# Loading and normalising the first token block tile by tile, with identity products ahead of it and another order of the first projections

## Chip, cores and metric

The kernel runs on one core of one Trainium2 chip. The metric is the device time of one execution in microseconds (us). The time of the kernel before is the median of three runs.

## What is computed

A sandwich of a differential-attention layer and a feed-forward layer over 2048 tokens of width 256, all in float32. Cut to what matters here:

```python
x = x + layernorm(attention(layernorm(x)))
x = x + layernorm(ffn(layernorm(x)))

# attention, 16 query heads and 8 key heads of width 128, in pairs
q, k, v = split(h @ Wqkv.T + b)
p = softmax(causal(q1 @ k1.T)) - lam * softmax(causal(q2 @ k2.T))
lam = exp(sum(lq1 * lk1)) - exp(sum(lq2 * lk2)) + LAMBDA_INIT
o = rmsnorm(p @ v) * subln_w * (1 - LAMBDA_INIT)
return concat(o) @ out_w.T + out_b
```

The change is in the first tenth of the kernel: the first layer norm, and the projections to q, k and v of the first tokens.

## The kernel before

The 16 query heads are worked in four groups g of four, each with two key heads and one value head of width 256. Tokens come in four blocks b (or nb) of 512, each of four tiles t of 128. For each block the kernel loads `xt` (128 partitions, 4 tiles, 256 columns), normalises it in place (`norm_in`, L462), turns it with eight TensorE transposes into `xnT` (`turn_in`, L468), and projects it: `project_heads` (L166) makes two heads of 512 tokens, `project_values` (L196) the values. In `project_heads` part 0 and part 1 are the query heads, part 2 the two key heads; `put_block` (L725) calls the values part 3.

A layer norm is `rstd_of` (L84): `bn_stats` and `bn_aggr` on VectorE for each tile (L89, L90), one addition of eps for all (L92), one power of -1/2 on GpSimd for all (L94). Then `normalise` (L97, L98) subtracts and scales tile by tile on VectorE.

In `turn_in` the eight transposes (L475) write one PSUM tile `pst`; ScalarE copies its first half (L476), then VectorE its second (L477).

**PSUM buffers.** Projections, turned tokens and scores share one pool `ps_s` of three buffers (tag "sc"), taken in turn: whatever is made first in the code gets the next buffer, and waits until the tile made three places earlier has been read. Projections of q and k are read by ScalarE (L192, with `both=False` both halves), those of v by VectorE (L209), scores by VectorE (L270, L281).

**Attention.** A `Unit` is one pair of heads for one tile of 128 queries. Short units (i under 8) hold two half tiles of queries (`subs` 0 and 1), and `scores(u, half)` works them in two halves; unit 0 has scores of 64 keys in its first half and of 128 in its second, unit 1 of 192 and 256. After the scores come exponentials on ScalarE (L298), the combination of the two maps (L325), which needs the scalar `nlam`, a transpose through DRAM (L347, L349, L359), and products with v three steps later (L371).

**What sets the order.** `manual_schedule` is on: each engine executes its instructions in the order in which the Python code issues them, and waits at each for its inputs. The main loop takes one unit a step. Projections and norms are hung into it by `put` into four dictionaries: `before` (ahead of the step's scores), `mid` and `between` (in this order, after the first half of the scores and its exponentials, ahead of the second half) and `after`. Step 0 reads in the kernel before:

```python
put(before, 0, norm_in, 0)
put(before, 0, load_lambdas)
put(before, 0, turn_in, 0)
put_block(before, [0] * 2, 0, 0, [2, 0], both=False)
put(before, 0, norm_in, 1)
put(before, 0, turn_in, 1)
put_block(before, [0] * 2, 0, 0, [1, 3], both=False)
put(before, 0, norm_in, 2)
```

**Loads.** SyncE's queue issues the four `xt` loads of 512 KB (L457); the fourth has to wait until the first buffer is free. ScalarE's queue issues the weights of group 0 (`load_qkv`, L131): two pieces of q, then k, then v, of 256 KB each (L137, L141). GpSimd's queue issues the columns of constants (L459), the bias of v (L142), and, in `load_lambdas` (L481 to L487), the lambda vectors `lt`, the output weights `wo` and two constants. `lambdas` (L489) works out `nlam`: VectorE multiplies and sums, ScalarE takes two exponentials (L498), VectorE subtracts (L499) and scales `wo` (L157). In the kernel before it stands after the values of block 1.

A matmul of the program in float32 stands in the profile as two TensorE instructions, a transpose as one: four matmuls of `project_heads` are eight records of L174, eight transposes of `turn_in` eight records of L475.

Of the kernel before, what the change touches and what calls it, by code (L numbers as in the profile page):

```python
# [10 lines left out]
F32 = mybir.dt.float32  # L11
# [5 lines left out]
P = 128  # L17
# [13 lines left out]
LAMBDA_INIT = 0.8 - 0.6 * math.exp(-0.3 * 1)  # L31
SCALE = D ** (-0.5)
LAG = 3
MASKED = -1e30
LOWEST = -3e38

# [10 lines left out]
def kernel(  # L47
# [16 lines left out]
    nc = tc.nc  # L64

    const = ctx.enter_context(tc.tile_pool(name="const", bufs=1))
    ident = const.tile([P, P], F32, name="ident")
    make_identity(nc, ident)
    hadm = const.tile([P, P], F32, name="hadm")

    make_causal_mask(nc, hadm, MASKED)
    mask = const.tile([P, 64], F32, name="mask")
# [11 lines left out]
    def rstd_of(pool, src, n, tag):  # L84

        st = pool.tile([P, 4, 6], F32, tag="st" + tag, name="st" + tag)
        mv = pool.tile([P, 4, 2], F32, tag="mv" + tag, name="mv" + tag)
        for t in range(n):
            nc.vector.bn_stats(st[:, t, :], src[t] if isinstance(src, list) else src[:, t, :])  # L89
            nc.vector.bn_aggr(mv[:, t, :], st[:, t, :])  # L90
        ve = pool.tile([P, 4], F32, tag="ve" + tag, name="ve" + tag)
        nc.vector.tensor_scalar(ve[:, :n], mv[:, :n, 1], EPS, None, ALU.add)  # L92
        rstd = pool.tile([P, 4], F32, tag="rs" + tag, name="rs" + tag)
        nc.gpsimd.tensor_tensor(rstd[:, :n], ve[:, :n], mhalf[:, :n], ALU.pow)  # L94
        return mv, rstd

    def normalise(dst, src, mv, rstd, t):  # L97
        nc.vector.tensor_scalar(  # L98
            dst, src, mv[:, t, 0:1], rstd[:, t : t + 1], ALU.subtract, ALU.mult
        )  # L100

    x4 = x.rearrange("(b t p) d -> b p t d", p=P, t=4)
# [5 lines left out]
    with ExitStack() as actx:  # L108
# [6 lines left out]
        ps_s = actx.enter_context(tc.tile_pool(name="ps_s", bufs=3, space=PSUM))  # L115
# [12 lines left out]
        wsrc = wqkvT.rearrange("(c p) o -> p c o", p=P)  # L128
        loaded = {}

        def load_qkv(g, engine, pieces=1):  # L131

            wq = xtp.tile([P, 2, 1024], F32, tag="wq", name=f"wq_{g}")
            vb = xtp.tile([P, 256], F32, tag="vb", name=f"vb_{g}")
            step = 512 // pieces
            for lo in range(0, 512, step):
                engine.dma_start(  # L137
                    wq[:, :, lo : lo + step], wsrc[:, :, g * 512 + lo : g * 512 + lo + step]
                )
            for lo, at in ((512, 2048 + g * 256), (768, 3072 + g * 256)):  # L140
                engine.dma_start(wq[:, :, lo : lo + 256], wsrc[:, :, at : at + 256])  # L141
            nc.gpsimd.dma_start(vb, vbias[:, ts(g, 256)].to_broadcast([P, 256]))  # L142
            loaded[g] = wq, vb

# [308 lines left out]
        xsm = pstack.enter_context(tc.tile_pool(name="xsm", bufs=2, side="right"))  # L453
        xts = []
        for b in range(NB):
            xt = xin.tile([P, 4, HID], F32, tag="xt", name=f"xt_{b}")
            nc.sync.dma_start(xt, x4[b])  # L457
            xts.append(xt)
        nc.gpsimd.dma_start(colv, cols)  # L459
        load_qkv(0, nc.scalar, pieces=2)  # L460

        def norm_in(b):  # L462
            xt = xts[b]
# [215 lines left out]
        def ffn_pieces():  # L679
            for b in range(NS - 1, -1, -1):  # L680
                prev, nxt = b + 1 < NS, b > 0
                if nxt:
                    load_x(b - 1)
                yield hidden(b, 0)
                if nxt:
                    front2(b - 1)
                if prev:
                    yield back(b + 1)
                    finish1(b + 1)
                    finish2(b + 1)  # L690
                yield hidden(b, 1)
                if nxt:
                    front3(b - 1)
                yield hidden(b, 2)
                if nxt:
                    turn_ffn(b - 1)
                    if b > 1:
                        front1(b - 2)
                yield hidden(b, 3)
            back(0)  # L700
            for lo in range(2):
                finish1(0, lo, 1)
                finish2(0, lo, 1)

        pieces = ffn_pieces()
# [14 lines left out]
        before, mid, between, after = {}, {}, {}, {}  # L720

        def put(where, step, f, *args, **kw):
            where.setdefault(step, []).append(lambda: f(*args, **kw))

        def put_block(where, steps, g, nb, parts, both=True):  # L725
            for step, part in zip(steps, parts):
                if part == 3:
                    put(where, step, project_values, g, nb)
                else:
                    put(where, step, project_heads, g, nb, part, both=both)  # L730


        put(before, 0, norm_in, 0)
        put(before, 0, load_lambdas)
        put(before, 0, turn_in, 0)
        put_block(before, [0] * 2, 0, 0, [2, 0], both=False)
        put(before, 0, norm_in, 1)
        put(before, 0, turn_in, 1)
        put_block(before, [0] * 2, 0, 0, [1, 3], both=False)
        put(before, 0, norm_in, 2)  # L740
        put_block(mid, [0] * 2, 0, 1, [0, 1], both=False)
        put(between, 0, turn_in, 2)
        put_block(between, [0] * 2, 0, 1, [2, 3], both=False)
        put(between, 0, lambdas)
        put(mid, 1, norm_in, 3)
        put_block(mid, [1] * 2, 0, 2, [0, 1], both=False)
        put_block(between, [1, 1], 0, 2, [2, 3], both=False)
# [3 lines left out]
        for g in range(1, NG):  # L751
            end = place[g, NT - 1, 0]
            put(after, end - 12, load_qkv, g, nc.sync)
            put(after, end + LAG + 2, load_wo, g)
            put(mid, end + LAG + 3, scale_wo, g)
            if g == 1:

                for nb in range(3):
                    put_block(between, [end + 5 - 2 * nb, end + 6 - 2 * nb], g, nb, [0, 1])
                put_block(before, [end] * 2, g, 3, [0, 1])  # L760
                for nb in range(4):
                    put_block(before, [end], g, nb, [2])
                    put_block(after, [end + 2], g, nb, [3])
            else:
                put_block(between, [end - 5, end - 4, end - 4, end - 3], g, 3, range(4))
                put_block(between, [end - 3, end - 3, end - 2, end - 2], g, 2, range(4))
                put_block(between, [end - 2, end - 1, end - 1], g, 1, range(3))
                put_block(after, [end - 1, end], g, 1, [3])
                put_block(before, [end], g, 0, [2])
                put_block(between, [end, end + 1], g, 0, [0, 1])  # L770
                put_block(after, [end + 2], g, 0, [3])
# [17 lines left out]
        for where, step, count in (  # L789
            *((between, last - 4 + j, 1) for j in range(4)),  # L790
            *((w, last + j, 1) for j in range(LAG + 3) for w in (before, between)),
            (after, last + LAG + 3, 6 * NS),
        ):
# [3 lines left out]
        at = lambda k: units[k] if 0 <= k < len(units) else None  # L797
        for step in range(len(units) + LAG + 4):
            for f in before.get(step, ()):
                f()  # L800
            new, mixed = at(step), at(step - 1)
            ripe, out1, out2, out3, out4 = (at(step - LAG - k) for k in range(5))
            if new:
# [96 lines left out]
```

## Time and profile before

| | us |
|---|---|
| median of three runs | 1495.02 |
| lowest and highest | 1494.45, 1495.09 |
| the profiled execution's own time | 1495.16 |
| its span, first to last instruction | 1493.4 |
| TensorE busy | 1454.7 (97%) |
| VectorE busy | 1080.2 (72%) |
| ScalarE busy | 498.3 (33%) |
| GpSimd busy | 285.4 (19%) |
| 16 DMA engines, queue of SyncE | 58.8% of the span |

A profile line of the timeline has: start in us from the span's start, length, engine and line, operation, output and inputs, how many instructions were merged, and in brackets the idle time of that engine before it and what ended it. PE is TensorE's matmuls, PEld its weight loads, DVE VectorE, ACT ScalarE, POOL GpSimd, SP SyncE; a q after the name is the engine's queue. The line of a table by stretches has: the stretch, its length, each engine's busy time with its number of instructions, the granted share of TensorE's clock, the DMA engines' share and GB/s. Ends of matmuls are modelled, so starts are the safer reading. The records of the granted clock begin in this trace at 17.13 us; earlier stretches are given as 1.00 for lack of a record.

### The profile page before, as it was taken

To read this page: it belongs to the slowest core of one execution; us is meant where nothing else is said; L and a number is where in the kernel's file an instruction comes from. 1 tells how busy PE (TensorE), PEld (TensorE's weight loads), DVE (VectorE), ACT (ScalarE), POOL (GpSimd) and SP (SyncE) were. 2 spreads that over 40 slices of the span, in tenths; PEclk is the share of its full clock that TensorE was granted. 3 is DMA by queue.
4 is the path that set the end of the run, shared out by engine and by line. 5 is a ranking of instruction groups with operands and counts; after the bars stand their busy time and mean duration, and the time that the engine had idled before them with its cause. 6 is when DMAs were issued, how large, how long until landed. Compare 5 with 4: busy or idle time off the path is not lost.

```text
span 1493.4 us, 17588 instructions
## 1 busy us (share of the span) xinstructions
PE 1454.7 (97%) x5464; PEld 1038.3 (70%) x5464; DVE 1080.2 (72%) x2825; ACT 498.3 (33%) x1011; POOL 285.4 (19%) x376
## 2 busy tenths in 40 slices
PE   6899999999999999999999999999999999999998
PEld 3457767666767777675677776665776666888887
DVE  3479788756666888654978788547898888866674
ACT  1354333323223334332333333324323233541211
POOL 2013222101111122111311121112221221222110
PEclk9999999999999999999999999999999999999999
DMA  3038998865366897831798888523997768622000
GB/s 115 8 93 185 186 207 171 170 127 121 77 136 151 168 201 158 164 78 50 167 180 175 172 193 178 110 64 84 245 189 159 157 160 164 144 79 64 24 26 15
DMA packets 463789, 198.41 MB, mean 133 GB/s; under 512 B 366128, under 2 KB 460864, under 8 KB 463696
## 3 DMA queue, kind: packets, MB, share of 16 engines
q1 hardware_dynamic: 459856, 187.62, 58.8%
q0 software_dynamic: 2592, 8.48, 2.1%
q10 hardware_dynamic: 1248, 1.18, 0.2%
q8 instruction: 45, 0.74, 0.2%
q14 instruction: 48, 0.39, 0.1%
HBM read 104.95 MB, written 92.27 MB: 132 GB/s over the span
## 4 chain that ended last, share of the span: by engine, by line
PE 87%; DVE 11%; issue 1%; ACT 1%; DMA 0%; POOL 0%; POOLq 0%; DVEq 0%; ACTq 0%
PE po L371 28%; PE sc L260 26%; PE pp L174 11%; PE pout L438 7%; PE gu L628 7%; PE pv L202 4%; PE pd L658 4%; DVE e L270 3%; DVE e L325 2%; DVE e L347 1%; DVE e L281 1%; DVE xo L417 0%; DMA xt<-in_x 0%; PE tx L615 0%; DVE nb L293 0%
## 5 line engine op out<-in xcount | busy, mean ns | idle before, releaser
L260 PE MATMUL sc<-k,q 128*128 128x512 f32 (+7 forms) x1280 | 481.6, 522 | 16.3 <-DVE last L281 8.9
L371 PE MATMUL po<-v,pt 128*128 128x256 f32 x2176 | 485.5, 379 | 0.0
L371 PEld LDWEIGHTS po<-v,pt 128*128 128x128 f32 x2176 | 425.7, 196 | 57.2 <-issue 10.0
L260 PEld LDWEIGHTS sc<-k,q 128*128 128x128 f32 x1280 | 237.2, 191 | 239.7 <-issue 191.7
L298 ACT ACTIVATE e<-e,nb 128x192 f32<-128x192 f32 (+28 forms) x256 | 299.5, 1170 | 302.2 <-DVE u L395 172.6
L270 DVE TENSOR_SCALAR_CACHE_REDUCE e<-sc 128x1024 f32<-128x1024 f32 (+14 forms) x248 | 231.5, 934 | 157.1 <-PE sc L260 156.4
L399 POOL TENSOR_TENSOR f<-u,mhalf 128x1 f32<-128x1 f32 (+1 forms) x96 | 59.3, 618 | 946.8 <-DVE u L395 644.7
L382 ACT COPY osb<-po 128x256 f32<-128x256 f32 (+1 forms) x96 | 42.6, 444 | 427.3 <-PE po L371 427.3
L174 PE MATMUL pp<-xnT,wq 128*128 128x512 f32 x384 | 174.5, 604 | 5.9 <-ACT xnT L476 3.0
L347 DVE STREAM_TRANSPOSE e<-e 128x768 f32<-128x768 f32 (+7 forms) x192 | 172.4, 937 | 7.1 <-DVE e L325 0.5
L401 POOL TENSOR_SCALAR osb<-osb,f 128x256 f32<-128x256 f32 x128 | 172.1, 1350 | 9.5
L325 DVE SCALAR_TENSOR_TENSOR e<-e,cf,e 128x64 f32<-128x64 f32 (+31 forms) x128 | 170.6, 1353 | 3.4
L174 PEld LDWEIGHTS pp<-xnT,wq 128*128 128x128 f32 x384 | 73.6, 194 | 90.9 <-issue 79.4
L438 PE MATMUL pout<-wo,oT 128*128 128x256 f32 x512 | 121.0, 379 | 0.0
L270 DVE TENSOR_SCALAR_CACHE_REDUCE e<-sc,mx 128x192 f32<-128x192 f32 (+13 forms) x136 | 100.5, 739 | 22.9 <-PE sc L260 9.1
L438 PEld LDWEIGHTS pout<-wo,oT 128*128 128x128 f32 x512 | 97.4, 190 | 12.8
L281 DVE CUSTOM_DVE_ANT_0 e<-sc,mask,mx 128x64 f32<-128x64 f32 x248 | 70.5, 284 | 8.9
L641 ACT ACTIVATE hT<-gu,colv 128x256 f32<-128x256 f32 x64 | 30.3, 474 | 133.7 <-PE gu L628 89.6
L628 PE MATMUL gu<-fxnT,wgate 128*128 128x256 f32 x256 | 65.8, 380 | 0.2 <-DVE last L281 0.2
L628 PE MATMUL gu<-fxnT,wup 128*128 128x256 f32 x256 | 65.7, 379 | 0.0
L642 DVE SCALAR_TENSOR_TENSOR hT<-gu,colv,hT 128x256 f32<-128x256 f32 x64 | 30.9, 482 | 40.0 <-ACT hT L641 39.9
L202 PE MATMUL pv<-wq,xnT 128*128 128x256 f32 x256 | 57.5, 380 | 0.2 <-DVE last L281 0.2
(103 smaller groups left out, 933.3 us busy)
## 6 DMA issues: line engine op xcount, KB each, us to landing
dr<-e SPq DMA_DIRECT2D x20, 1024.0 KB, 4.7
pt<-dr SPq DMA_DIRECT2D x80, 256.0 KB, 5.6
dr<-e SPq DMA_DIRECT2D x20, 896.0 KB, 4.3
pt<-dr SPq DMA_DIRECT2D x80, 224.0 KB, 5.1
do<-xo SPq DMA_DIRECT2D x64, 256.0 KB, 2.4
oT<-do SPq DMA_DIRECT2D x256, 64.0 KB, 2.7
dr<-e SPq DMA_DIRECT2D x20, 768.0 KB, 4.0
pt<-dr SPq DMA_DIRECT2D x80, 192.0 KB, 4.6
```

Source lines behind the costliest of these rows:

```text
L174: nc.tensor.matmul(pp[:, ts(h, 512)], lhsT=wq[:, c, ts(j, P)], rhs=xnT[:, c, cols4], start=(c == 0), stop=(c == 1),)
L202: nc.tensor.matmul(pp[:, ts(t, 256)], lhsT=xnT[:, c, ts(nb * 4 + t, P)], rhs=wq[:, c, 768:1024], start=(c == 0), stop=(c == 1),)
L260: nc.tensor.matmul(sc[:, lo : lo + ww], lhsT=qT[m][:, u.i, u.subs[a]].rearrange("d p q -> d (p q)"), rhs=kT[m][:, at + lo : at + lo + ww], ...
L270: nc.vector.tensor_scalar(e[:, at : at + full], sc[:, :full], 1.0, best, ALU.mult, ALU.max, accum_out=u.mx[:, k0, c : c + 1],)
L281: nc.vector.tensor_tensor_reduce(e[:, L - 64 : L], sc[:, full : full + 64], mask, 1.0, best, ALU.add, ALU.max, accum_out=u.last[:, k0 : k0 ...
L298: nc.scalar.activation(e, e, AF.Exp, bias=u.nb[:, 2 * a + m : 2 * a + m + 1], scale=SCALE, accum_out=u.d[:, a, m : m + 1],)
L325: nc.vector.scalar_tensor_tensor(e0, e1, cf[:, a : a + 1], e0, ALU.mult, ALU.add)
L347: nc.vector.transpose(xv[:, r], ev[:, r])
L371: nc.tensor.matmul(u.po[:, ts(a, HID)], lhsT=ptv[:, g, r, :], rhs=vt[:, kc, :], start=(kc == 0), stop=(kc == u.i),)
L401: nc.gpsimd.tensor_scalar(u.osb[:, a, :], u.osb[:, a, :], f[:, a : a + 1], None, ALU.mult)
L438: nc.tensor.matmul(u.pout[:, :HID], lhsT=u.oT[:, c, p, :], rhs=wos[u.g][:, p, c, :], start=(p == 0 and c == 0), stop=(p == 1 and c == 1),)
L628: nc.tensor.matmul(ps[:, ts(2 * j + n, 256)], lhsT=ffn[which][:, c, ts(fc, P)], rhs=xnT[:, c, :], start=(c == 0), stop=(c == 1),)
```

## The change

The first block comes in four transfers of 128 KB (one tile each), two from SyncE's and two from ScalarE's queue, and the weights of group 0 are issued behind them on ScalarE's queue. `load_qkv` issues k first, then q, then v, in all groups. The first block is normalised by `norm_first`: statistics, addition and power for each tile alone, with the normalisation of a tile issued after the statistics of the next. `warm_up` multiplies the identity with itself twelve times into a buffer of `ps_s` that nothing reads. In step 0, `lambdas` comes after the norm of block 1 and ahead of part 1 of q; `turn_in` of block 1 comes after part 1 instead of ahead of it; the values of block 0 and the norm of block 2 come after the first scores.

```diff
+WARM = 12
...
-            for lo in range(0, 512, step):
-                engine.dma_start(
-                    wq[:, :, lo : lo + step], wsrc[:, :, g * 512 + lo : g * 512 + lo + step]
-                )
-            for lo, at in ((512, 2048 + g * 256), (768, 3072 + g * 256)):
-                engine.dma_start(wq[:, :, lo : lo + 256], wsrc[:, :, at : at + 256])
+            parts = [(512, 2048 + g * 256, 256)]
+            parts += [(lo, g * 512 + lo, step) for lo in range(0, 512, step)]
+            parts += [(768, 3072 + g * 256, 256)]
+            for lo, at, n in parts:
+                engine.dma_start(wq[:, :, lo : lo + n], wsrc[:, :, at : at + n])
...
-            nc.sync.dma_start(xt, x4[b])
+            if b:
+                nc.sync.dma_start(xt, x4[b])
+            else:
+
+                for t in range(4):
+                    (nc.sync, nc.scalar)[t % 2].dma_start(xt[:, t, :], x4[0][:, t, :])
+                load_qkv(0, nc.scalar, pieces=2)
             xts.append(xt)
         nc.gpsimd.dma_start(colv, cols)
-        load_qkv(0, nc.scalar, pieces=2)
+
+        def warm_up():
+
+            warm = ps_s.tile([P, 1024], F32, tag="sc", name="warm")
+            for k in range(WARM):
+                nc.tensor.matmul(warm[:, :P], lhsT=ident, rhs=ident, start=True, stop=True)
+
+        def norm_first():
+
+            xt = xts[0]
+            done = None
+            for t in range(4):
+                ln = rstd_of(xsm, xt[:, t : t + 1, :], 1, f"x{t}")
+                if done:
+                    normalise(xt[:, t - 1, :], xt[:, t - 1, :], *done, 0)
+                done = ln
+            normalise(xt[:, 3, :], xt[:, 3, :], *done, 0)
...
-        put(before, 0, norm_in, 0)
+        put(before, 0, warm_up)
+        put(before, 0, norm_first)
         put(before, 0, load_lambdas)
         put(before, 0, turn_in, 0)
         put_block(before, [0] * 2, 0, 0, [2, 0], both=False)
         put(before, 0, norm_in, 1)
+        put(before, 0, lambdas)
+        put_block(before, [0], 0, 0, [1], both=False)
         put(before, 0, turn_in, 1)
-        put_block(before, [0] * 2, 0, 0, [1, 3], both=False)
-        put(before, 0, norm_in, 2)
+        put_block(mid, [0], 0, 0, [3], both=False)
+        put(mid, 0, norm_in, 2)
         put_block(mid, [0] * 2, 0, 1, [0, 1], both=False)
         put(between, 0, turn_in, 2)
         put_block(between, [0] * 2, 0, 1, [2, 3], both=False)
-        put(between, 0, lambdas)
```

## The prediction

> **What bounds the kernel now.** I read the table of stretches first: from 100 us on TensorE is busy 99 us in 100, so what the first 55 us lose is lost for good, and what they win shifts the rest. There I read the timeline, by engine. First the start:
>
> ```profile
> 0.73 11.41 SPq L457 DMA_DIRECT2D xt<-in_x  x4
> 5.64 0.43 DVE L89 BATCH_NORM_STATS2 stx<-xt 128x6 f32<-128x256 f32 x1 [5.64 <-DMA xt<-in_x]
> 7.90 0.17 DVE L92 TENSOR_SCALAR vex<-mvx 128x4 f32<-128x4 f32 x1
> 8.23 1.05 POOL L94 TENSOR_TENSOR rsx<-vex,mhalf 128x4 f32<-128x4 f32 x1 [4.82 <-DVE vex L92]
> 9.31 1.45 DVE L98 TENSOR_SCALAR xt<-xt,mvx,rsx 128x256 f32<-128x256 f32 x4 [1.24 <-POOL rsx L94]
> 9.78 1.97 PE L475 MATMUL pst<-ident,xt 128*128 128x128 f32 x8 [9.78 <-DVE xt L98]
> 11.78 0.58 ACT L476 COPY xnT<-pst 128x512 f32<-128x512 f32 x1 [6.92 <-PE pst L475]
> 12.42 9.45 PE L174 MATMUL pp<-xnT,wq 128*128 128x512 f32 x16 [0.68 <-ACT xnT L476]
> ```
>
> A strict chain: the block lands at 5.62, norm, transposes, copy, and the first projection starts at 12.42. Next, TensorE's clock, from the weight loads:
>
> ```profile
> 16.00 0.33 PEld L174 LDWEIGHTS pp<-xnT,wq 128*128 128x128 f32 x1 [0.52 <-issue]
> 16.85 0.33 PEld L174 LDWEIGHTS pp<-xnT,wq 128*128 128x128 f32 x1 [0.52 <-issue]
> 17.42 0.19 PEld L174 LDWEIGHTS pp<-xnT,wq 128*128 128x128 f32 x1 [0.24 <-issue]
> 17.85 0.19 PEld L174 LDWEIGHTS pp<-xnT,wq 128*128 128x128 f32 x1 [0.24 <-issue]
> ```
>
> Starts lie 0.85 us apart until 17.13 (the first clock record) and 0.43 after it: half a clock for 4.7 us of projections, a loss of 2.35. Then TensorE's own order, with the waits in brackets:
>
> ```profile
> 21.71 1.04 PE L475 MATMUL pst<-ident,xt 128*128 128x128 f32 x8
> 30.95 3.70 PE L174 MATMUL pp<-xnT,wq 128*128 128x512 f32 x8 [0.93 <-DVE v L209]
> 36.00 3.70 PE L174 MATMUL pp<-xnT,wq 128*128 128x512 f32 x8 [1.35 <-DVE last L281]
> 48.78 0.59 PE L260 MATMUL sc<-k,q 128*128 128x192 f32 x2 [0.87 <-DVE v L209]
> 51.43 0.98 PE L260 MATMUL sc<-k,q 128*128 128x192 f32 x2 [2.06 <-DVE e L270]
> ```
>
> Each is a wait for a PSUM buffer that VectorE has still to read: 5.21 us. At 36.00 VectorE reads the first scores late, since the norm of block 2 is queued ahead of them; at 51.43 `lambdas` is. The last wait also costs clock (0.59 us busy in 3.35, then 0.50 granted):
>
> ```profile
> 47.91:51.26 3.35, 0.59 (x2) 0.30 (x2) 3.01 (x12) 0.20 (x1) 0.00 (x0) 1.00 0.00 0
> 51.26:54.67 3.41, 3.24 (x5) 1.82 (x6) 3.06 (x22) 1.86 (x8) 0.00 (x0) 0.50 0.01 2
> ```
>
> That is 3.24/2 = 1.62 more.
>
> **What the Trainium skill says.** "TensorE: Matmul & The Clock Gate", Part 1, section "What's actually happening": the array runs at half rate until a free-running window of about 3.4 us was busy, and falls back after an idle one. The trace agrees: the slow stretch is 3.41 long, 17.13 and 51.26 are ten such stretches apart. How busy a window must be isn't said; here 17% lost the clock. The same page, Part 4, says that transposes don't count as busy in the same way; no run so far tests that. "DMA: Bandwidth & Descriptors", section "Issuing engines are not separate DMA queues": transfers of all queues share the same 16 engines, so two queues save issue time only. The trace agrees: one issue takes about 0.5 us, and block and weights land together (5.62, and 5.3 for the first weights).
>
> **The change, part by part.**
>
> *Four transfers.* The DMA view gives 83, 60 and then about 350 GB/s in slices of 0.75 us from 1.5 us on, so 107 KB by 3.0 us; 131 KB, one tile, is there at 3.1. The whole block lands 0.5 to 0.8 us after its bytes can have moved (block plus first weights, 786 KB, are there at 4.9). I take 3.9 for the landing of tile 0, range 3.6 (alone) to 4.3 (tile 1 shares the engines). Tiles 1 to 3 follow within 1.2 us at that rate and are needed 0.8, 2.0 and 3.1 later: covered. k's 256 KB are behind 512 KB on the two queues, some 8 us, and needed at 10.4: 2.4 us of cover.
>
> *Norm by tile.* From the block's rows statistics to aggregate takes 0.46, aggregate to addition 0.22, addition to the next statistics 0.12. The power of one column stands at the kernel's end:
>
> ```profile
> 1484.65 0.15 DVE L92 TENSOR_SCALAR vec<-mvc 128x1 f32<-128x1 f32 x1
> 1484.95 0.55 POOL L94 TENSOR_TENSOR rsc<-vec,mhalf 128x1 f32<-128x1 f32 x1 [12.97 <-DVE vec L92]
> 1485.53 0.54 DVE L98 TENSOR_SCALAR y<-pd,mvc,rsc 128x256 f32<-128x256 f32 x1 [0.73 <-POOL rsc L94]
> ```
>
> so addition to normalisation takes 0.88. After tile 0 lands, its normalisation starts at 1.60 (behind tile 1's statistics), each next at 1.16 more (0.36 + 0.46 + 0.22 + 0.12): 2.76, 3.92; the last waits for its own power, 3.12 + 0.68 + 0.88 = 4.68. In the block it was 9.31 + 3×0.36 − 5.62 = 4.77: four powers instead of one eat the overlap. What is won is that only two transposes are left: 0.47 to the first (as 9.31 to 9.78), 0.21 + 0.42 at half clock, 0.67 for the copy. The first projection starts at 3.9 + 4.68 + 0.47 + 0.63 + 0.67 = 10.35, against 12.42: **2.07**.
>
> *Identities.* 12 products are 24 records. At half clock transposes of this size come 0.21 apart (8 in 1.97, the last 0.42 long), so 5.1 us, from 1.45 (identity ready, after POOL's masks) to 6.6; the first transposes are due at 5.97 and the last pair at 9.05, so this is hidden. Upper bound: 0.33 each, the weight load's length at half clock: 7.9, to 9.4. What they buy is open: between 7.5 and 10.35 only four transposes run, so a clock won at 7 can be lost again. I value the identities at nothing, with one slow stretch of 3.4 us from the first projection, 1.7; bounds 0 (clock held) and 2.6. Sixteen records at full clock took 21.71 − 12.42 − 2.35 = 6.94; turn of block 1 or part 1 can follow at 10.35 + 6.94 + 1.7 = 18.99 instead of 21.71. With the landing: **2.7**, of which 0.65 is clock.
>
> *New order.* Let E be the end of part 1 (18.99 + 3.43 = 22.4).
> - Transposes of block 1 run from E to E+0.87. ScalarE copies q's halves at E+0.2 to 1.46 (1.26 for two), then `pst` to 2.05; VectorE's half ends at 2.75. First scores: the second needs q's other half, 0.2 us idle. Values need the buffer of `pst` (three places back): 2.85 instead of 1.88, 0.97 idle. This is new; part 1 covered it before.
> - VectorE reads the first scores right behind that copy (E+3.1), so both waits in front of block 1's queries (0.93, 1.35) go. The norm of block 2 runs on VectorE from E+7.7 to 12.6; its transposes are due at 13.2: covered by 0.6.
> - `lambdas` (2.1 us of VectorE) moves behind the norm of block 1, near 16. It waits for ScalarE's exponential, which is behind the copies of part 0, E−2.0; done at E−0.8, and VectorE owes nothing until E+2.05: 2.8 us of cover. Its loads stay behind the powers on POOL: the fourth starts at 8.5, as the one did at 8.23, so they land as before (lt 4.5 after issue, wo 5.3: by 15). `lambdas`' going leaves the wait at 48.78 (0.87) and nearly removes the next: 0.1. With 2.06 less idle, TensorE keeps its clock.
>
> Before 5.21 + 1.62 = 6.83; after 0.2 + 0.97 + 0.87 + 0.1 = 2.14: **4.7**. The part loaded first in later groups comes 12 steps ahead: nothing.
>
> Sum 2.7 + 4.7 = 7.4. The profiled execution took 1495.16 (1493.4 span, 1.76 around it): 1487.8. It stands 0.14 above the median of 1495.02: **1487.6**.
>
> **Rivals.**
> 1. The clock holds from the identities to the projections: 1.7 more, 1485.9. For: 5 us of products fill a window. Against: little runs between 7.5 and 10.35.
> 2. The first block gains little: identities at 0.33 end at 9.4, eight transposes follow at 0.21, the first projection starts near 12.0; or tile 0 lands with the old block, 5.62, and it starts at 12.07. 7.4 − 1.7 = 5.7: 1489.3. Against: SyncE's first bytes move by 2 us.
> 3. The clock drop moves instead of going: another wait (71.01 to 73.39 is 2.4 us idle) falls into a window whole. 7.4 − 1.6 = 5.8: 1489.2. The windows are free-running, so this is chance; the drop at 1252.75 may as well vanish.
> 4. Slower: `lambdas` now stands on VectorE ahead of block 1's copy and all scores. If lt or wo landed late, everything would queue behind. Its cover ends if wo lands after about 23.5; to eat 7.4 it must land after 31, against 15 before. That decides from 16 us of delay.
>
> **Numbers.** Forecast 0.50 (own range 1486.3 to 1488.8), rival 1 0.20, rivals 2 and 3 together 0.24, change without effect 0.04, rival 4 0.02. The range runs from clock held and tile 0 at 3.6 with a little spared later (1485.1) to rivals 2 or 3 with a late landing (1490.2). A measurement tells 0.2%, 3.0 us, from no change; all but the last two cases lie beyond: faster 0.94, same 0.04, slower 0.02.
>
> **What would show it.** First statistics near 3.9 and first projection near 10.35; weight loads 0.85 apart for four records there, then 0.43; a wait of about 1 us ahead of the values of block 0, none ahead of block 1's queries, unit 1's second scores close behind its first and no clock drop there. A first projection at 12, or a drop that stands elsewhere, would make me wrong by 1.7; a wait on VectorE's `lambdas` for a DMA would by more.

## The result, and the profile after

| | before | changed |
|---|---|---|
| median of six runs each, us | 1495.16 | 1488.29 |
| lowest to highest | 1494.45 to 1496.82 | 1485.62 to 1489.19 |
| the profiled execution's own time | 1495.16 | 1489.19 |
| its span | 1493.4 | 1487.4 |

The ratio is 0.9948 with a 95% interval of 0.9935 to 0.9961: 6.9 us less. The forecast was 1487.6. The two profiled executions differ by 6.0 (the changed one is the slowest of its six), and these 6.0 can be followed from start to end. First the timeline of the changed kernel at its start, in the order of the data:

```profile
1.46 4.28 PE L471 MATMUL warm<-ident 128*128 128x128 f32 x24 [1.46 <-POOL ident masks.py:199]
3.95 0.43 DVE L90 BATCH_NORM_STATS2 stx<-xt 128x6 f32<-128x256 f32 x1 [3.95 <-DMA xt<-in_x]
8.53 0.41 DVE L99 TENSOR_SCALAR xt<-xt,mvx,rsx 128x256 f32<-128x256 f32 x1 [0.44 <-POOL rsx L95]
9.48 0.59 ACT L498 COPY xnT<-pst 128x512 f32<-128x512 f32 x1 [2.05 <-PE pst L497]
10.36 2.15 PE L174 MATMUL pp<-xnT,wq 128*128 128x512 f32 x3 [0.92 <-DMA wq<-in_wqkvT]
```

The first statistics start at 3.95 instead of 5.64, the last normalisation 4.58 later, the first projection at 10.36 instead of 12.42. Its bracket names what came last: a DMA, k's weights, not ScalarE's copy. The copy of `xnT` started 0.64 ahead of the first projection in the kernel before (11.78 to 12.42); by that measure the projection could have started at 10.12, and the weights cost 0.24 here.

Next the table of stretches of the changed kernel; the share of the clock is the column after the five engines:

```profile
7.71:11.13 3.42, 1.65 (x6) 0.89 (x7) 1.48 (x4) 0.59 (x1) 3.05 (x5) 1.00 1.07 346
11.13:14.54 3.41, 3.41 (x5) 1.33 (x4) 2.26 (x9) 0.00 (x0) 0.55 (x1) 0.50 1.03 343
65.74:69.15 3.41, 3.28 (x4) 1.50 (x5) 1.01 (x4) 0.08 (x1) 0.15 (x1) 0.50 0.23 77
```

The records of the granted clock in this trace begin at 4.30, while the identities ran: full clock from there. It was lost again at 11.13, after a window in which TensorE ran the last transposes and 0.77 us of projections, and came back 3.41 later. It was lost once more at 65.74, after a wait that the change does not touch. TensorE's timeline shows where that is:

```profile
25.15 3.72 PE L202 MATMUL pv<-wq,xnT 128*128 128x256 f32 x16 [0.77 <-DVE xnT L499]
28.71 7.03 PE L174 MATMUL pp<-xnT,wq 128*128 128x512 f32 x16
...
44.82 1.12 PE L260 MATMUL sc<-k,q 128*128 128x192 f32 x4 [0.87 <-DVE v L209]
45.85 10.54 PE L174 MATMUL pp<-xnT,wq 128*128 128x512 f32 x24
...
62.46 1.04 PE L497 MATMUL pst<-ident,xt 128*128 128x128 f32 x8
65.87 2.07 PE L174 MATMUL pp<-xnT,wq 128*128 128x512 f32 x2 [2.37 <-ACT xnT L498]
```

One wait is new (0.77 ahead of block 0's values). The queries of block 1 (28.71) follow without a wait, and so do the second scores of unit 1 (44.82, four records in one group). Blocks 2 and 3 start at 45.85 and 65.87 instead of 52.20 and 73.39. The same two starts, in TensorE's timeline of the kernel before:

```profile
52.20 8.26 PE L174 MATMUL pp<-xnT,wq 128*128 128x512 f32 x16
...
73.39 3.78 PE L174 MATMUL pp<-xnT,wq 128*128 128x512 f32 x8 [2.37 <-ACT xnT L476]
```

So the account of the two traces is: 2.71 less at the end of the first sixteen projection records (19.00 for 21.71; the end is taken as the start of the record behind them), 7.52 less at block 3 (the kernel before had paid its clock drop at 51.26 by then), and 6.0 less at the end. The difference of 1.5 is the drop at 65.74, which the trace before does not have.

### The profile page after: what moved, and what is told of

Read it like the earlier page. It is cut to its first block, busy times and chain, and to the rows that moved or that the text cites. A ratio compares the mean times of both kernels' runs of the same rounds, so it can differ in the third digit from the quotient of the medians.

```text
span 1487.4 us, 17643 instructions
## 1 busy us (share of the span) xinstructions
PE 1458.2 (98%) x5488; PEld 1040.3 (70%) x5488; DVE 1080.8 (73%) x2828; ACT 498.6 (34%) x1011; POOL 287.1 (19%) x379
## 4 chain that ended last, share of the span: by engine, by line
PE 86%; DVE 11%; DMA 1%; issue 1%; ACT 1%; ACTq 0%; SPq 0%; POOL 0%; POOLq 0%; DVEq 0%
PE po L371 28%; PE sc L260 25%; PE pp L174 11%; PE gu L650 7%; PE pout L438 7%; PE pd L680 4%; PE pv L202 4%; DVE e L270 3%; DVE e L325 2%; DVE e L347 2%; DVE e L281 1%; DMA wq<-in_wqkvT 1%; DVE xo L417 0%; PE tx L637 0%; DVE nb L293 0%
## 5 line engine op out<-in xcount | busy, mean ns | idle before, releaser
L371 PEld LDWEIGHTS po<-v,pt 128*128 128x128 f32 x2176 | 425.3, 196 | 57.6 <-issue 10.2
```

The costliest lines, as they stand in the source:

```text
L371: nc.tensor.matmul(u.po[:, ts(a, HID)], lhsT=ptv[:, g, r, :], rhs=vt[:, kc, :], start=(kc == 0), stop=(kc == u.i),)
```

## The experiments

Unless a table says otherwise, the edit is made to the changed kernel, and everything is still computed. "Block 2" and "block 3" are the starts of their first projections, as above. The medians with an interval were taken against the kernel before on the same chip.

**The head alone, the order alone.** `e1_head` keeps loads, norm and identities of the change, and takes step 0 of the kernel before:

```diff
-put(before, 0, norm_in, 0)
+put(before, 0, warm_up)
+put(before, 0, norm_first)
```

> The changed head (four transfers, norm by tile, identities, k's weights first) with the old order of step 0. If head and order add up, the first projection starts at 10.4 us and the turn of block 1 at 19.0 instead of 21.7, the four waits for PSUM buffers (5.2 us together) and a clock drop behind the last of them come back, and the time is about 2.7 us under the kernel before: near 1492.4. Rival: the earlier start is given back at the old waits (VectorE's norm of block 2 and lambdas are late anyway); then the first projection is early but the projections of block 2 start within 0.5 us of the 52.2 of before, and the time is that of before.

`e2_order` is the kernel before with the other half:

```diff
 put(before, 0, norm_in, 1)
+put(before, 0, lambdas)
+put_block(before, [0], 0, 0, [1], both=False)
 put(before, 0, turn_in, 1)
-put_block(before, [0] * 2, 0, 0, [1, 3], both=False)
-put(before, 0, norm_in, 2)
+put_block(mid, [0], 0, 0, [3], both=False)
+put(mid, 0, norm_in, 2)
...
-put(between, 0, lambdas)
```

> The old head with the new order of step 0. If they add up: first projection at 12.4, part 1 starting at 21.7, a wait of about 0.8 ahead of the values of block 0, none at block 1's queries, projections of block 2 starting near 48.6 instead of 52.2 and at full clock, so 4.7 to 4.9 us under before, near 1490.3; 1.6 more where a clock drop falls into another wait. Rival: the order pays only with the early head, because lambdas then waits for its loads or the norm of block 2 is late; then a new wait on VectorE of over 1 us stands in the first 50 us and the gain is under 3.

| | first projection | 16 records done | block 2 | block 3 | median us | ratio to before, interval |
|---|---|---|---|---|---|---|
| before | 12.42 | 21.71 | 52.20 | 73.39 | 1495.16 | |
| changed | 10.36 | 19.00 | 45.85 | 65.87 | 1488.29 | 0.9948, 0.9935 to 0.9961 |
| e1_head | 10.29 | 18.72 | 49.15 | 71.63 | 1493.09 | 0.9975, 0.9967 to 0.9983 |
| e2_order | 12.35 | 21.08 | 47.93 | 67.95 | 1490.78 | 0.9966, 0.9953 to 0.9978 |

By the medians the two halves add up within their intervals: 0.25% and 0.34%, against 0.52% together. At block 2 they seem to give too much, 3.05 from the head and 4.27 from the order, where the change has 6.35. The surplus of 0.97 lies at the start, where the first stretch of half clock fell otherwise: e1 has its sixteen records done 0.28 ahead of the changed kernel, e2 0.63 ahead of the kernel before. Behind the sixteen records the parts separate cleanly. In e1 the stretch from there to block 2 is 30.43 long, as before (30.49), with nearly the same waits in it (0.93, 1.28, 0.87, 2.06): a head gained 3 us early is not eaten at the next wait. In e2 it is 26.85, exactly that of the changed kernel. To block 3 it is 51.68 in the kernel before, and 46.87 in both the changed kernel and e2. So the order brings 4.81, and the remaining 2.71 of the 7.52 stand at the end of the sixteen records.

**What in the order counts.** `e4_lambdas_back` puts `lambdas` back to where the kernel before had it:

```diff
-put(before, 0, lambdas)
...
 put_block(between, [0] * 2, 0, 1, [2, 3], both=False)
+put(between, 0, lambdas)
```

> The changed kernel with lambdas back at its old place, behind the values of block 1. Theory: VectorE does its 2.1 us of lambdas between the values of block 1 and unit 1's scores again, so the wait in front of unit 1's second scores comes back at about 2.0 us, and the projections of block 2 start at 47.9 instead of 45.85; where a clock window holds that wait whole, the clock drops behind it (1.6 more). Rival: the norm of block 2, not lambdas, makes that wait; then it stays under 0.3 and the start is 45.9.

TensorE's timeline of e4:

```profile
45.31 0.98 PE L260 MATMUL sc<-k,q 128*128 128x192 f32 x2 [2.06 <-DVE e L270]
46.08 11.63 PE L174 MATMUL pp<-xnT,wq 128*128 128x512 f32 x24
```

The wait of 2.06 is back, to the hundredth, and the stretch from the sixteen records to block 2 is 29.25 instead of 26.85: 2.4 more. Near the end of the wait the clock fell, at 45.0, as it had at 51.26 in the kernel before; that is why the 24 records from 46.08 take 11.63 instead of 10.54. A single run took 1488.99 us beside 1494.73 of the kernel before. That is no worse than the changed kernel although a wait of 2 us is back, because in this run the clock held from 7.45 to 45.0, the sixteen records were done at 16.83, and no drop fell at block 3.

`e8_values_ahead` puts the values of block 0 ahead of the first scores again:

```diff
-put_block(mid, [0], 0, 0, [3], both=False)
+put_block(before, [0], 0, 0, [3], both=False)
```

> The changed kernel with the values of block 0 ahead of the first scores again, but behind the turn of block 1, and the norm of block 2 still behind the scores. Theory: the values behind the scores bring nothing themselves: ahead, their own wait (0.77) goes, and a wait of 0.9 for VectorE's reading of them stands before block 1's queries; the 1.3 us wait for the scores stays away, since that was the norm of block 2. Projections of block 2 start at 45.7 to 46.0, less what the clock does at the start. Rival: the values' place is what pays, both old waits (0.9 and 1.3) come back and block 2 starts at 47 or later.

```profile
29.05 7.13 PE L174 MATMUL pp<-xnT,wq 128*128 128x512 f32 x16 [0.93 <-DVE v L209]
```

This is TensorE's timeline of e8 at block 1's queries: the wait of 0.93 that the change had removed is back, and the one of 0.77 that it had brought is gone. From the sixteen records to block 2 it takes 26.49, against 26.85. Behind or ahead of the scores, the values cost one wait of this size. The 1.28 to 1.35 of the kernel before are gone in e8 too: that is the work of the norm of block 2 alone, which stands behind the first scores in both.

**The loads and the norm.** `e6_one_transfer` and `e7_block_norm` undo one each:

```diff
 # e6
-for t in range(4):
-    (nc.sync, nc.scalar)[t % 2].dma_start(xt[:, t, :], x4[0][:, t, :])
+nc.sync.dma_start(xt, x4[0])
```

```diff
 # e7
-put(before, 0, norm_first)
+put(before, 0, norm_in, 0)
```

> The changed kernel, but the first block comes in one transfer of 512 KB on SyncE's queue, with the weights beside it from the start; norm by tile and all else as changed. Theory: splitting the transfer is what makes the head earlier: the first statistics start at 5.6 instead of 3.95, the first projection at about 12.0 instead of 10.36, and part 1 ends 1.0 to 2.4 later (the clock moves with it). Rival: norm by tile makes the head earlier; then the first projection stays within 0.6 us of 10.4.

> The changed kernel with the block norm (one addition and one power for all four tiles) on the four transfers. Theory: the tiles land within 0.8 us, and the block norm takes as long from the first tile as the norm by tile (4.7 against 4.6 us), so the last normalisation ends at about 9.0 and the first projection still starts where k's weights land, 10.2 to 10.4. Rival: norm by tile is worth about 1 us; then the first projection starts at 11.2 or later.

With one transfer the first statistics start at 5.55 and the first projection at 11.71; a single run took 1493.17 us. That time does not price the transfers alone: the clock was lost at 11.0 for two stretches, the sixteen records were done at 21.70, and drops followed at 69.0 and 598. With four transfers and the norm of the whole block, the start of e7 is, in the timeline of TensorE:

```profile
7.55 1.48 PE L497 MATMUL pst<-ident,xt 128*128 128x128 f32 x8 [1.47 <-DVE xt L99]
9.71 10.57 PE L174 MATMUL pp<-xnT,wq 128*128 128x512 f32 x24 [0.68 <-ACT xnT L498]
```

The first statistics of e7 started at 3.42, and the copy of `xnT` 5.65 later; in the changed kernel the copy starts 5.53 behind the statistics. Beside the identities, the norm tile by tile is worth 0.1 us. Without them it is worth 0.37 (5.77 in e3 below, 6.14 in the kernel before), since the slow transposes then no longer stand in a row; both together bring 0.6. The small transfers bring the larger part (first statistics at 5.55 in e6, at 3.95 in the changed kernel). In e7 the eight transposes stood together, the clock was full from 5.02 past the first projections, and a single run took 1486.45 us.

**The identities and the clock.** `e3_no_identities` leaves them out; `e5_fill` puts 11 more products of the identity behind the transposes of the four tiles, into the same buffer that nothing reads:

```diff
 # e3
-put(before, 0, warm_up)
```

```diff
 # e5, in turn_in, behind the two transposes of tile t
+if b == 0:
+    fill((3, 3, 2, 3)[t])
```

> The changed kernel without the twelve identity products; all else the same. Theory: they buy little, since the clock they win at 4.3 us is lost at 11.1, 0.8 us into the projections: without them the last transposes take 0.25 longer, the first projection starts at 10.3 to 10.6 (it waits for k's weights anyway), all of it at half clock until a busy window ends: 0.4 to 1.3 us slower than the changed kernel, near 1489. Rival 1: they carry the head's gain, 2 us or more lost. Rival 2: nothing at all, within 0.3 us at the start of part 1.

> The changed kernel with eleven more identity products, put behind the transposes of each tile of block 0 (3, 3, 2, 3), so that TensorE is busy for most of the time up to the first projection. Theory: the clock drop at 11.1 comes from the nearly idle stretch before it, so it goes: the projections run at 0.43 us from the first on, part 1 starts at 17.3 instead of 19.0, time 1.7 us under the changed kernel, near 1486.6. Rival: products of the identity don't keep the clock, or the products delay the transposes: part 1 still starts at 19 or later.

Without identities the sixteen records were done at 19.18 (changed: 19.00), and the median is 1489.09, ratio 0.9950 (0.9936 to 0.9963). In this pair of traces the twelve products bring 0.2 us, less than the first statistics differ from one execution to the next (3.95 and 3.47), and the medians show no difference. That is no fixed price: in the changed kernel their clock is lost before the projections profit, but of the eight traces with these twelve products and four transfers it held through the sixteen records in three (e4, e7, e12), which had them done at 16.66 to 16.83, and was lost in five, at 18.72 to 20.77. With 23, TensorE's timeline reads

```profile
10.19 10.57 PE L174 MATMUL pp<-xnT,wq 128*128 128x512 f32 x24
20.59 1.04 PE L502 MATMUL pst<-ident,xt 128*128 128x128 f32 x8
```

24 records in 10.57 instead of 12.23: no drop at the start, sixteen records done at 17.16, block 2 at 44.01, both 1.84 earlier. The median, 1488.40 with ratio 0.9944 (0.9931 to 0.9956), does not show it. In its trace two drops stand later, at 64.64 and at 593.70, where the changed kernel's trace had one, at 65.74 (each has a further one near 1245). In this one trace, what the start gains and the later windows cost are of the same size.

**Other waits, and the weights.** `e10_turn_early` moves the turn of block 3 from step 2 into step 1, behind block 2's values and ahead of the scores, so that its copy is done when the projections of block 3 are due:

```diff
-put(mid, 2, turn_in, 3)
...
 put_block(between, [1, 1], 0, 2, [2, 3], both=False)
+put(between, 1, turn_in, 3)
```

> The changed kernel with the turn of block 3 moved from step 2 to step 1, behind the values of block 2. Theory: the 2.37 us wait at 63.5 us, and the clock drop that starts in it, come from ScalarE's copy of that block being queued behind unit 2's exponentials; placed earlier the copy is done in time, block 3's first projection starts near 62.7 instead of 65.9, no drop at 65.7: 2.5 to 3.2 us, and 1.6 more in executions that had the drop there. Rival: unit 2's first scores or the projection then wait for VectorE's copy instead, and under 1.5 us is won.

```profile
63.89 1.47 PE L260 MATMUL sc<-k,q 128*128 128x320 f32 x4 [0.26 <-DVE xnT L499]
65.20 3.24 PE L174 MATMUL pp<-xnT,wq 128*128 128x512 f32 x7
```

In TensorE's timeline of e10 the wait of 2.37 is gone (0.26 is left ahead of the scores), block 3 starts 17.58 behind block 2 instead of 20.02, and no drop stands near it. The median is 1484.12 (1483.71 to 1487.88), ratio 0.9928 (0.9915 to 0.9940). It is the fastest version with more than one run. The changed kernel on the same chip (e13 below) took 1488.94, so this is 4.8 less, of which the 2.44 between the two blocks are seen in the trace; the profiled execution is the slowest of the five, and what the others saved beyond that was not traced.

`e11_all` joins e5 and e10, and puts eight products of the identity behind the transposes of the feed-forward layer of the last group of blocks (`whole` is the PSUM tile that `tx` is half of), where all traces have a wait of 2.4 and a clock drop near 1245:

```diff
+for k in range(8 if b == NS - 1 else 0):
+    nc.tensor.matmul(whole[:, 512:640], lhsT=ident, rhs=ident, start=True, stop=True)
```

> The changed kernel with the eleven identity products between the first tiles, the early turn of block 3, and eight identity products behind the first transposes of the feed-forward, where TensorE waits 2.36 us at 1243.5. Theory: three clock drops go (11.1, 65.7 and 1246.8), together with most of the wait at 63.5: 1.7 + 2.5 to 3.2 + about 1.5 us under the changed kernel in the trace, near 1482.5. Rival: products that nobody reads don't hold the clock at 1243, or delay the scores behind them: no gain beyond the sum of the first two, near 1484.

```profile
1240.81 0.78 PE L260 MATMUL sc<-k,q 128*128 128x320 f32 x2 [0.57 <-DVE last L281]
...
1244.51 4.97 PE L260 MATMUL sc<-k,q 128*128 128x320 f32 x12 [1.89 <-ACT fxnT L649]
```

It missed: 1486.18 (1484.99 to 1487.17), ratio 0.9937 (0.9923 to 0.9950), not better than e10. The timeline of TensorE shows two losses. The wait ahead of 1240.81 is short now, but a new one of 1.89 stands three scores on, and the clock fell at 1244.3 all the same; from block 3 to the end it takes 1421.9, against 1420.0 in traces whose only drop is the one near 1245. And k's weights made the first projection late by 1.4 (11.13). Why the scores at 1244.51 wait for the copy of `fxnT`, which the changed kernel does not show, stays open.

`e12_bias_late` issues the bias of v of group 0 with the loads of the lambdas, behind the powers on GpSimd's queue (8.02 instead of 1.66); `e13_changed_again` is the changed kernel once more.

```diff
 def load_qkv(g, engine, pieces=1):
...
-    nc.gpsimd.dma_start(vb, vbias[:, ts(g, 256)].to_broadcast([P, 256]))
+    if g:
+        load_vb(g, vb)
...
 def load_lambdas():
+    load_vb(0, loaded[0][1])
```

> The changed kernel with the load of v's bias on GpSimd's queue moved from 1.7 us to behind the powers of the first norm. Theory: its 128 KB in 4 KB packets, moved beside the tokens and weights from 3.75 to 7.5 us, hold DMA engines and are why these stretches run at 230 GB/s instead of 361; then k's weights land by about 8.5 instead of 10.2 and the first projection waits only for the copy. Rival: the small transfers themselves are slower to feed; the rate stays under 280 and k's weights land at 10 or later.

> The changed kernel once more, as it is, to stand beside the two others on one chip. Expected 1486 to 1489 with the number of clock drops behind the start (none to three) setting which; if the drops are set by where the waits fall in free-running windows, this trace's drops lie elsewhere than at 11.1, 65.7 and 1246.8 while the starts up to the first drop agree within 0.5 us. Rival: the drops belong to the program and stand at the same places.

The first projection in TensorE's timeline, of e13 and then of e12:

```profile
11.01 13.31 PE L174 MATMUL pp<-xnT,wq 128*128 128x512 f32 x24 [2.05 <-DMA wq<-in_wqkvT]
```

```profile
9.69 10.57 PE L178 MATMUL pp<-xnT,wq 128*128 128x512 f32 x24 [0.68 <-ACT xnT L502]
```

The copy of `xnT` started at the same time in both (8.99 and 9.05), so that both first projections could start near 9.7. In e13 k's weights held it back by 1.4 us; in e12 nothing did, the clock held, and block 3 started at 63.53. In e12 the weights landed at 8.9, later than the 8.5 expected and well ahead of the rival's 10; the rate, 281 as shown below, lies just above the 280 that the rival named. A single run of e12 took 1485.36 us. The same program as the changed kernel, e13, measured 1488.94 (1488.05 to 1491.90), ratio 0.9957 (0.9944 to 0.9969), and its trace has drops at 9.8 (two stretches long), 67.8 and 596.9 beside the one near 1245. The one at 67.8 stands in the same wait as that at 65.74, ahead of block 3:

```profile
67.58 5.40 PE L174 MATMUL pp<-xnT,wq 128*128 128x512 f32 x8 [2.36 <-ACT xnT L498]
```

The one at 596.9 has no fellow in the changed kernel's trace. One program does not have one set of drops: the rival that they belong to the program falls.

## Why the prediction was right, and which step failed

**Right.** The sum was 7.4; the traces show 7.52 at the start of block 3. The end of the sixteen records was put at 18.99 (19.00), E at 22.4 (22.43), the landing of the first tile at 3.9 (3.95), its norm at 4.68 (4.58). The wait ahead of block 0's values was put at 0.97 and is 0.77: the copies end 2.72 behind E, not 2.85. The waits in front of block 1's queries and of unit 1's second scores went, and 0.87 stayed. The move of `lambdas` cost nothing: `nlam` was ready at 20.6, ahead of E. e4 confirms its price alone (2.06 with nothing left over), e2 that of the whole order. The order was put at 4.7 and brings 4.81, and that is solid: from the sixteen records to block 3 it takes 46.86 to 46.88 in every trace that has the whole new order and no other change behind the sixteen records.

**Where luck helped.** That the head came out at 2.71 for 2.7, and the sixteen records at 19.00 for 18.99, is luck. The prediction charged one slow stretch, 1.7, from the first projection. In the profiled execution one stretch was lost, but it began 0.77 later. The same program had the sixteen records done at 20.72 in e13, with two stretches lost from 9.77 and k's weights late, so that only 0.99 of the head's gain was left and block 3 stood 5.81 ahead of the kernel before, not 7.52. In e12, with the clock held, the sixteen records were done at 16.66. The prediction's bounds for this term, 0 and 2.6, are what the traces come near to: 0 in e4, e7 and e12, 2.8 in e13.

**Rival 3 happened in the profiled execution.** The drop did move, to the very wait that the prediction named (2.37 here), and cost the 1.5 between 7.52 and 6.0. The other five executions took 1485.62 to 1488.56, with a mean granted clock of 0.995 to 0.998; they were not traced, so that the drop stood elsewhere in some of them is inferred. Rival 1, that the clock holds, did not happen in the two traces of this program (changed, e13); it did in e4, e7 and e12, without an edit meant for it, and in e5. "The Trainium skill", page "TensorE: Matmul & The Clock Gate", Part 1, section "What's actually happening", has a free-running window of about 3.4 us; these traces agree: ahead of the one that the end of each trace cuts off, every drop is 3.41 long or twice that. The page has the clock fall back after an idle window; here windows that were half busy lost it too, and the measurement decides. The prediction had only the 17% of the kernel before. No limit comes out of these traces: with TensorE busy for 1.65 of 3.42 us (changed, from 7.71), 1.80 of 3.41 (e1, from 6.47) and 1.82 of 3.42 (e10, from 6.14) the clock was lost, with 1.56 (e7, from 59.63) and 1.70 of 3.41 (e4, from 65.48) it was kept. The ends of matmuls are modelled, and most of the busy time is transposes in the windows of e1, e10 and e7, on both sides of the line; what decides stays open.

**The step that failed:** "k's 256 KB are behind 512 KB on the two queues, some 8 us, and needed at 10.4: 2.4 us of cover". They landed at 10.2, and between 9.3 and 11.3 in the other traces with four transfers and an early bias; in seven of these ten traces, the changed kernel's among them, the projection waited for them, by 0.2 to 1.7 us beyond the copy. In the changed kernel's trace that was 0.24, and two errors of the other sign hid it: the norm chain was 0.1 shorter, and the last transposes ran at full clock (0.48 from their start to the copy instead of 0.63). In e13 it was 1.4. The step took the rate of the kernel before. The DMA view from 3.75 to 7.5 us, of before, changed and e12, has in its lines the packets with the mean rate, and the share that GpSimd's queue q0 took of the 16 engines:

```profile
DMA packets 1368, 1.35 MB, mean 361 GB/s; under 512 B 70, under 2 KB 1363, under 8 KB 1368
...
q0 software_dynamic: 25, 0.04, 4.0%
```

```profile
DMA packets 790, 0.86 MB, mean 230 GB/s; under 512 B 41, under 2 KB 759, under 8 KB 790
...
q0 software_dynamic: 47, 0.13, 26.7%
```

```profile
DMA packets 1065, 1.05 MB, mean 281 GB/s; under 512 B 46, under 2 KB 1065, under 8 KB 1065
...
q0 software_dynamic: 32, 0.03, 9.5%
```

The bias of v was issued at 2.85 in the kernel before and at 1.66 in the changed one, a side effect of calling `load_qkv` earlier in the code. In the stretch in which k's weights move, the 47 packets of GpSimd's queue, the bias for the most part, took time that adds up to 26.7% of the engines for 0.13 MB. With it out of the way (e12) the rate was 281, k landed at 8.9, and the wait was gone. Both lie outside what the ten traces with the early bias show, 160 to 250 GB/s and 9.3 to 11.3, so that the bias matters is well supported, though e12 is one trace. "The Trainium skill", page "DMA: Bandwidth & Descriptors", section "Issuing engines are not separate DMA queues", says that the queues share the 16 engines; e12 fits that. But the share of packet time is no price: e8, the slowest of the ten at 160 GB/s, and e10 at 178 have the two smallest shares of q0, 16.3% and 14.1%, while e3, the fastest at 250, has 26.4%. Nor is the bias the whole cause: 281 is not 361, and e6, with one transfer in place of four and the bias as early, moved 342 GB/s and had k's weights (issued first, at 0.73) landed by 5.2. That points to the small transfers themselves costing rate, above all together with the early bias; e3, e5 and e7 were not held up by the weights without the edit of e12, and how the loss divides stays open.

**What the prediction left unvalued.** It gave the identities nothing, and they bring 0.2 in one pair of traces; where the clock held with them, the sixteen records took 6.97 from the first projection (e7, e12) instead of 8.84 (e3). It gave the norm by tile 0.35 from the landing to the first projection (6.80 to 6.45, of which 0.09 in the norm and the rest in the transposes); without identities it brings that, 0.37 from the statistics to the copy, and beside them 0.1. It did not price the drops near 594, which the trace before does not have. Priced by the time from block 3 to the end: 1420.0 with the drop near 1245 alone (before, e12), 1421.0 with one near 594 as well (e2, e7, e10), 1421.55 with one near 65 instead (changed), 1422.6 and 1422.5 with all three (e5, e13). That is 1.0 and 1.5 to 1.6 each, more than the norm by tile brings, and not far below the 2.44 that the turn of e10 saves. A version with the turn of e10, the bias of e12 and the norm of e7 was not run.

## What to carry to other kernels

Sum a change of order from the waits of TensorE's own timeline, and check the sum at a point just behind the change rather than at the end. Here the sum for the order held to 0.1 us in trace after trace. The sum for the head came out in one execution and was 1.7 us off in another of the same program, and the end carried 1 to 3 us of clock drops that no edit decided: one trace that fits does not confirm a term that such drops can move. When a load is issued earlier, list what else its function issues, on the other queues too. And of three steps that look alike at the start of a kernel (small loads, norm by tile, warming), measure each alone: here the small loads brought most of the early start.

## What the runs showed of the hardware

- ScalarE had issued four transfers by 2.16 us in the changed kernel; the fifth, the second piece of q's weights, was not issued before 4.14, 0.02 after the first of its own four had landed (4.12). In e12 and e13 it is the same: 3.72 behind 3.70, 3.65 behind 3.63. That the landing released it is inferred. The load of ScalarE's function table, which stands behind these issues, moved from 3.33 (e6, with four transfers on this queue) to 6.14. It was hidden here.
- The same program landed k's weights at 10.2 in one execution and at 10.9 in another, and its first statistics started at 3.95 and 3.47.
- Products of 128 columns start 0.21 us apart at half clock and 0.11 at full clock (24 records from 1.46 to 5.74, the clock rising at 4.30).
